# A four-layer graph network: the last attention layer in 32-column tiles, and a moved blank write

## Chip, core and metric

The kernel runs on one core of a Trainium2 chip. The metric is the time of one launch on the device, in microseconds. The core has five engines with an instruction queue each: TensorE (PE, matmuls, with weight loads shown as PEld), VectorE (DVE), ScalarE (ACT), GpSimd (POOL) and SyncE (SP). SP, ACT and POOL also issue DMA transfers, in the order in which these stand in their queues.

## What is computed

3125 nodes with 256 features pass through four layers; each adds a graph step and a mixing step to the nodes, then a feed-forward step. The change touches the end: the feed-forward step of layer 2, which picks two of eight experts for all nodes from the mean of the features, and layer 3. The reference of layer 3, cut:

```python
xn = _layernorm(x)
x = x + relu(gat(xn, edge_index, W, att_src, att_dst)) + mix(xn)
x = x + experts(x)          # one of 8 experts per node, with a capacity

def gat(x, edge_index, W, att_src, att_dst):
    xp = (x @ W).reshape(n, 4, 64)
    e = leaky_relu(a_src[src] + a_dst[dst], 0.2)      # per edge and head
    e_exp = exp(e - segment_max(e, dst)[dst])
    alpha = e_exp / segment_sum(e_exp, dst)[dst]
    return segment_sum(alpha * xp[src], dst)          # 4 heads of 64
```

## The kernel before

The 3125 nodes lie in 25 blocks of 125 (`P`, `NB`). `PIECES` groups them in six pieces of 500 nodes (`PW`) and one of 125. All arithmetic named here is in f32. `bank()` hands out four PSUM banks in turn.

A scheduler orders the instructions of each engine from the order in the code and from priorities; a pool's buffers and data dependencies decide the waits.

**Layer 2's feed-forward** (`l2_ffn`, L1779). The mean over all nodes is reduced (L1789), multiplied by the router weight `wr` (L1794), two softmaxes and a top-2 on VectorE and ScalarE follow, SP loads the two expert numbers into registers, and then each expert's weights (L1821 to L1825). `expert` multiplies all nodes by them; `y` takes up each block's result on VectorE (L1018). `wr` is loaded by SP, behind the weights of layer 3's mix.

**The blank write** (`l3_ffn`, L2168 on). Layer 3's experts read their nodes from `bx`, a table in DRAM of 3912 slots of 514 values, 8 MB. Before anything is scattered to it, it is filled with blank rows (L2190 and L2192, on ScalarE's queue) from a buffer named `row`. The name has one buffer, which the router of layer 3 uses later; the first such use is a copy of the nodes' numbers into it (L2253), which has no other input and so may stand early in VectorE's queue.

**The graph layer** (`l3_dense`, L1915). The edges are kept as a table of counts, sources by targets. The attention weights of one block of sources and one head for up to 1000 targets (two pieces) are made densely: ScalarE computes `t` (L1965), VectorE multiplies by the counts `cs` and gives `z` (L1968). TensorE multiplies `z` with the block's features: the stationary operand is `xr`, 64 features of the head and a column of ones, 65 columns; it accumulates 65 rows by 500 targets in one bank per head and piece (L1971). The last row is the sum of the weights. A pass over the 25 blocks for two heads and two pieces is called a half-turn here; there are six, and one turn for the last piece with all four heads. One block of a half-turn is a step: two `t`, two `z`, four matmuls. After a half-turn the sums are copied out, turned with small transposes of 65 rows (L1987), and per block divided and added to `x` (`finish`, L1925 to L1932).

`z` has three buffers, `t` two, `cs` three. The four banks of the accumulators are used again by the next half-turn.

**Beside it runs the mix** (`l3_mix_by_pieces`), interleaved by `together`, which always takes the part that has come less far. It is first keys and values for all blocks, then seven pieces of projections, normalisation and a small feed-forward part. When graph layer and mix have both finished a piece, `arrive` counts it down and calls `follow` (in `l3_ffn`, L2200 on), which normalises the nodes, routes them and scatters them to `bx` (L2255); the graph layer does so at step 5 of the next turn. Then the eight experts run.

Of the kernel before, what the change touches and what calls it, by code (L numbers as in the profile page):

```python
# [12 lines left out]
F32 = mybir.dt.float32  # L13
# [10 lines left out]
N = 3125  # L24
# [81 lines left out]
EARLY = 0.25  # L106
PIECES = [(i, min(PW, N - i)) for i in range(0, N, PW)]


class Net:  # L110
# [106 lines left out]

    def expect(self, parts, follow=None, lag=0):

        self.waiting = {i: parts for i, _ in PIECES}  # L220
        self.follow = follow or self.norm_turn_piece
        self.lag, self.due = lag, []

    def arrive(self, i):
        self.waiting[i] -= 1
        if self.waiting[i] == 0:
            self.due.append(i)
            while self.due and (len(self.due) > self.lag or not any(self.waiting.values())):
                i = self.due.pop(0)
                self.follow(i, min(PW, N - i))  # L230
# [1545 lines left out]
    def l2_ffn(self):  # L1776
        nc, tc, a = self.nc, self.tc, self.a
        NE = 8
        with ExitStack() as s:  # L1779
            sb = s.enter_context(self.pool("f2_sb"))  # L1780
            wk = s.enter_context(self.pool("f2_wk", 2))
            wr = self.load_w(sb, "L2_ffn_Wr")
# [35 lines left out]
            for j in range(2):  # L1818
# [6 lines left out]
                nc.sync.dma_start(b1, a["L2_ffn_b1"][ds(e, 1)].rearrange("o p f -> (o p) f"))  # L1825
# [11 lines left out]
    def l3_gnn_mix(self, before, arrivals):  # L1837
# [6 lines left out]
        with ExitStack() as s:  # L1844
# [12 lines left out]
            xr = sb.tile([P, NB, 4, 65], F32, name="xr")  # L1857
            nc.gpsimd.memset(xr[:, :, :, 64:65], 1.0)
            al = sb.tile([P, NB, 8], F32, name="al")
            for b in range(NB):  # L1860
                ps = self.bank()
                self.mm_tok(ps[:P, :264], self.xt, b, wx)
                nc.vector.tensor_copy(xr[:, b, :, :64], ps[:P, :D].rearrange("p (h d) -> p h d", h=4))
# [51 lines left out]
    def l3_dense(self, sb, wk, pa, xr, us, r_d):  # L1915

        nc = self.nc
# [3 lines left out]
        at = free[:65, 8 * PW:12 * PW].rearrange("p (h d) -> p h d", h=2)  # L1921

        def finish(b, h0, nh, acc):

            nc.vector.tensor_scalar(few[:, b, h0:h0 + nh], acc[:, :, 64], 1e-20, None, op0=OP.is_lt)  # L1925
            rd = wk.tile([P, 4], F32, name="rd")
            nc.vector.tensor_scalar(rd[:, :nh], acc[:, :, 64], 1e-20, None, op0=OP.max)
            nc.vector.reciprocal(rd[:, :nh], rd[:, :nh])
            t = wk.tile([P, 4, 64], F32, name="tf")
            nc.vector.tensor_mul(t[:, :nh], acc[:, :, :64], rd[:, :nh, None].to_broadcast([P, nh, 64]))  # L1930
            v = self.x[:, b, h0 * 64:(h0 + nh) * 64]
            nc.vector.scalar_tensor_tensor(v, t[:, :nh].rearrange("p h d -> p (h d)"), 0.0, v,  # L1932
                                           op0=OP.max, op1=OP.add)

        def target_rows(i, h0):

            n = min(2 * PW, N - i)
            for h in (h0, h0 + 1):
                if n > 0:
                    self.move(nc.sync, rows[:P, h, :n], r_d[h, i:i + n].partition_broadcast(P))  # L1940

        done, there = 0, []
        for h0 in (0, 2):
            target_rows(0, h0)
        for p0 in range(0, len(PIECES), 2):
            pcs = PIECES[p0:p0 + 2]
            n = sum(w for _, w in pcs)
            hg = 4 if n < PW else 2
            for h0 in range(0, 4, hg):
                acc = {}  # L1950
                for h in range(hg):
                    for k in range(len(pcs)):
                        acc[h, k] = pa.tile([65, 512], F32, name=f"acc{h * len(pcs) + k}")
                for b in range(NB):
                    cs = wk.tile([P, 2, PW], BF, name="cs", bufs=3)
                    if len(pcs) == 2:
                        self.move(nc.sync, cs, self.ctt_d[p0:p0 + 2, :, b, :].rearrange("k p d -> p k d"))
                        c = cs.rearrange("p k d -> p (k d)")
                    else:
                        self.move(nc.sync, cs[:, 0, :n], self.ctt_d[p0, :, b, :n])  # L1960
                        c = cs[:, 0, :n]
                    for h in range(hg):
                        k4 = h0 + h
                        t = wk.tile([P, 2 * PW], F32, name="t5")
                        nc.scalar.activation(t[:, :n], rows[:, k4, :n], AF.Relu, bias=us[:, 2, b, k4:k4 + 1],  # L1965
                                             scale=us[:, 0, b, k4:k4 + 1])
                        z = wk.tile([P, 2 * PW], F32, name="z", bufs=3)
                        nc.vector.scalar_tensor_tensor(z[:, :n], t[:, :n], us[:, 1, b, k4:k4 + 1], c,  # L1968
                                                       op0=OP.add, op1=OP.mult)
                        for k, (i, w) in enumerate(pcs):  # L1970
                            nc.tensor.matmul(acc[h, k][:, :w], xr[:, b, k4, :], z[:, k * PW:k * PW + w],  # L1971
                                             start=(b == 0), stop=(b == NB - 1))
                        done += n
                    yield done / (NB * N * 4)
                    if b == 5:
# [3 lines left out]
                if hg == 2:  # L1979
                    target_rows(pcs[0][0] + 2 * PW, h0)  # L1980
                    for h in range(2):
                        for k, (i, w) in enumerate(pcs):
                            self.evac(at[:, h, k * PW:k * PW + w], acc[h, k][:, :w])
                    for j in range(n // P):
                        ps = self.bank()
                        for h in range(2):
                            nc.tensor.transpose(ps[:P, h * 65:(h + 1) * 65], at[:, h, j * P:(j + 1) * P],  # L1987
                                                self.ident[:65, :65])
# [12 lines left out]
        for i in there:  # L2001
            self.arrive(i)
# [422 lines left out]
```

## Time and profile before

| | us |
|---|---|
| median of three runs | 4667.59 (4659.35 to 4668.40) |
| the profiled execution | 4666.18 |
| its span, first to last instruction | 4664.40 |

| stage of the profiled execution | us from the start |
|---|---|
| layers 0 to 2 up to the last gather matmul | 0 to 3251 |
| last transposes, mean, router, expert weights | 3251 to 3299 |
| layer 2's experts and layer 3's projections | 3299 to 3533 |
| graph layer 3 with its mix | 3533 to 4395 |
| its last turn, with 125 targets | about 4313 to 4395 |
| routing of the last piece, to the last scatter | 4395 to 4409 |
| layer 3's experts | 4409 to 4664 |

How to read the lines: a group has line, engine, operation, out<-in with shapes, count, then busy time, mean time of one, the idle time of the engine just before them and what released it. PE records of successive matmuls overlap, since a matmul's record reaches to its end while the next one has begun. A line of the windows has the stretch, its length, the busy time and count of each engine, the granted clock of TensorE, the share of DMA time and GB/s.

### The profile page before, as it was taken

How to read it: one execution, taken by the hardware profiler on the slowest of the kernel's cores; microseconds unless marked ns; L12 is line 12 of the kernel's file. 1: busy time of each engine (PE TensorE's matmuls, PEld its weight loads, DVE VectorE, ACT ScalarE, POOL GpSimd, SP SyncE). 2: the span in 40 equal slices, each digit the busy share in tenths (PEclk: the TensorE clock that was granted, in tenths of full speed). 3: DMA queues.
4: the chain of work that ended last, by engine and by line, in shares of the span. 5: the costliest groups of instructions: out<-in, count | busy, mean ns of one | idle time of the engine just before them, and what ended most of it. 6: DMA issues, size and time to landing. Idle time of an engine off the chain costs nothing. (4 is left out here: it accounts for less than half of the span.)

```text
span 4664.4 us, 50401 instructions
## 1 busy us (share of the span) xinstructions
PE 3722.3 (80%) x16695; PEld 2505.9 (54%) x16695; DVE 2505.6 (54%) x8604; ACT 1302.8 (28%) x2336; POOL 1020.2 (22%) x1041
## 2 busy tenths in 40 slices
PE   1887796499938799999656566766799999999698
PEld 0676695277724556555545455655464444444466
DVE  5877317544475526994322323444265666777544
ACT  1367100022213223323100000000155655555521
POOL 2000000400055000000577777775000000000011
PEclk9786896599959799999877777887899999999699
DMA  6244630244332000000333333334102222221232
GB/s 176 75 113 118 138 82 22 81 135 140 107 85 40 4 29 9 13 14 7 106 105 106 104 104 104 104 104 139 58 7 59 59 63 56 63 52 49 74 107 68
DMA packets 256035, 358.86 MB, mean 77 GB/s; under 512 B 62719, under 2 KB 199350, under 8 KB 255765
## 3 DMA queue, kind: packets, MB, share of 16 engines
q1 hardware_dynamic: 135900, 176.07, 13.1%
q0 software_dynamic: 62832, 126.93, 10.3%
q10 hardware_dynamic: 57033, 52.54, 4.2%
q8 instruction: 136, 2.23, 0.2%
q14 instruction: 134, 1.10, 0.1%
HBM read 268.73 MB, written 94.97 MB: 78 GB/s over the span
## 5 line engine op out<-in xcount | busy, mean ns | idle before, releaser
L1601 POOL DMA_INDIRECT hg<-hx_d,idx x782 | 743.3, 950 | 282.8 <-issue 214.2
L1617 PE MATMUL acc<-hg,to 128*125 128x256 f32 x2042 | 584.5, 449 | 197.9 <-DVE to L1612 192.8
L1617 PEld LDWEIGHTS acc<-hg,to 128*125 128x125 f32 x2042 | 455.4, 227 | 309.3 <-DVE to L1612 216.3
L1971 PE MATMUL acc<-z,xr 125*65 125x500 f32 (+1 forms) x1400 | 577.4, 556 | 14.3 <-DVE z L1968 13.0
L1965 ACT ACTIVATE t<-xn,us 125x1000 f32<-125x1000 f32 (+1 forms) x400 | 409.4, 1037 | 239.0 <-DVE z L1968 228.1
L1968 DVE SCALAR_TENSOR_TENSOR z<-t,us,cs 125x1000 f32<-125x1000 f32 (+1 forms) x400 | 409.3, 1028 | 115.5 <-PE acc L1971 92.6
L1971 PEld LDWEIGHTS acc<-z,xr 125*65 125x65 f32 x1400 | 188.9, 145 | 314.8 <-issue 265.5
L1605 DVE TENSOR_TENSOR kw<-hg,awt 128x8 f32<-128x8 f32 x98 | 16.4, 168 | 581.2 <-DMA hg<-hx_d,idx 513.2
L261 PE MATMUL ps<-xt,w 128*128 128x500 f32 (+1 forms) x672 | 269.0, 547 | 1.8 <-DMA w<-in_L_ffn_W_dram 1.8
L1612 DVE TENSOR_SCALAR to<-iota_w,rel_b,kw 128x125 f32<-128x125 f32 (+1 forms) x782 | 245.2, 383 | 35.6 <-PE acc L1617 28.7
L1536 DVE SCALAR_TENSOR_TENSOR junk<-iota_w,rel_b,lock 128x125 f32<-128x125 f32 (+1 forms) x782 | 248.1, 386 | 0.0
L2255 POOL DMA_INDIRECT bx_d<-row,slot x25 | 31.2, 1248 | 891.3 <-ACT t L1965 422.9
L589 PE MATMUL ps<-y,cb 125*125 125x256 bf16 x1875 | 214.7, 279 | 0.0
L589 PEld LDWEIGHTS <-cb 125*125 125x125 bf16 x1875 | 213.5, 141 | 0.1
L797 ACT ACTIVATE k<-k 125x128 f32<-125x128 f32 x50 | 15.9, 318 | 687.0 <-DVE k L796 686.9
L190 ACT ACTIVATE rstd_t<-rstd_t 125x4 f32<-125x4 f32 (+2 forms) x86 | 17.2, 203 | 645.8 <-DVE rstd_t L189 630.2
L255 PE MATMUL ps<-wo,h 128*125 128x256 f32 x800 | 187.7, 386 | 3.6 <-ACT h L1439 2.6
L243 PE MATMUL ps<-ident,xn 125*128 125x125 f32 x300 | 58.8, 347 | 159.8 <-DVE xn L209 159.7
L1445 DVE SCALAR_TENSOR_TENSOR x<-ps,lg,x 125x256 f32<-125x256 f32 x200 | 92.7, 480 | 173.6 <-PE ps L255 173.6
L261 PEld LDWEIGHTS ps<-xt,w 128*128 128x128 f32 x672 | 122.7, 193 | 114.7 <-issue 102.4
L261 PE MATMUL ps<-h,w 128*128 128x500 f32 (+1 forms) x448 | 179.5, 541 | 2.3 <-ACT h L1434 1.6
L255 PEld LDWEIGHTS ps<-wo,h 128*125 128x125 f32 x800 | 142.9, 187 | 65.9 <-ACT h L1439 43.7
(566 smaller groups left out, 6326.7 us busy)
## 6 DMA issues: line engine op xcount, KB each, us to landing
cs<-ctt_d SPq DMA_DIRECT2D x150, 218.8 KB
w<-in_L_ffn_w_dram SPq DMA_DIRECT2D x52, 512.0 KB
cnt_d<-cd SPq DMA_DIRECT2D x25, 683.6 KB
cb<-cnt_d SPq DMA_DIRECT2D x25, 683.6 KB
ctt_d<-ct ACTq DMA_DIRECT2D x6, 2734.4 KB
hg<-hx_d,idx POOLq DMA_INDIRECT x782, 2.8
b0x_d<-zero SPq DMA_DIRECT2D x1, 9984.0 KB
xb<-b0x_d SPq DMA_DIRECT2D x26, 384.0 KB
```

What stands on the lines that cost most here:

```text
L243: self.nc.tensor.transpose(ps[:, j * P:(j + 1) * P], src[:, i // P + j, h * 128:(h + 1) * 128], self.ident[:P, :P])
L255: self.nc.tensor.matmul(ps, xt[:, h, b * P:(b + 1) * P], w[:, h, :], start=(h == 0), stop=(h == k - 1))
L261: self.nc.tensor.matmul(ps, w[:, h, :], xt[:, h, i:i + n], start=(h == 0), stop=(h == k - 1))
L589: nc.tensor.matmul(ps[:P, :D], cf[k][:, h * P:(h + 1) * P], y3[:, b0 + k, j, :], start=(k == 0 and j == 0), stop=(k == m - 1 and j == 2))
L1445: nc.vector.scalar_tensor_tensor(self.x[:, b, :], ps[:P, :D], g[:, b, e:e + 1], self.x[:, b, :], op0=OP.mult, op1=OP.add)
L1536: nc.vector.scalar_tensor_tensor(junk[:, :m * P], self.iota_w[:, :m * P], rel[:, c:c + 1], lock[:, b:b + m].rearrange("p b n -> p (b n)"), ...
L1601: nc.gpsimd.indirect_dma_start(out=hg[:, j, :], out_offset=None, in_=hx, in_offset=bass.IndirectOffsetOnAxis(ap=idx[:, c0 + j:c0 + j + 1], ...
L1612: nc.vector.tensor_scalar(to, self.iota_w[:, :nb * P], rel[:, c:c + 1], kw[:, j:j + 1], op0=OP.is_equal, op1=OP.mult)
L1617: nc.tensor.matmul(acc[k], to[:, (k - b) * P:(k - b + 1) * P], hg[:, j, :D], start=(c == first[k]), stop=(c == last[k]))
L1965: nc.scalar.activation(t[:, :n], rows[:, k4, :n], AF.Relu, bias=us[:, 2, b, k4:k4 + 1], scale=us[:, 0, b, k4:k4 + 1])
L1968: nc.vector.scalar_tensor_tensor(z[:, :n], t[:, :n], us[:, 1, b, k4:k4 + 1], c, op0=OP.add, op1=OP.mult)
L1971: nc.tensor.matmul(acc[h, k][:, :w], xr[:, b, k4, :], z[:, k * PW:k * PW + w], start=(b == 0), stop=(b == NB - 1))
```

## The change

Transfers. The router weight of layer 2 is loaded by ScalarE's queue instead of SP's. The blank write becomes a function that is called in `l2_ffn` after the second expert's weights are issued, on SP's queue, with an order-only dependency that keeps it behind them. The second weight matrix of layer 3's expert 1 goes from ScalarE's queue to SP's.

Graph layer. The 65-column matmul with its column of ones is replaced. `xr` has 64 columns per head; each head's 64 columns are two tiles of 32, placed at columns 0, 32, 64, 96 of the array for two heads, so that one row of four matmuls gives the 128 outputs of two heads for one piece. A second row does the other piece. A third row of four has 32 columns of ones as stationary operand and gives the sums. A step is so 12 matmuls in three rows in place of 4, into three banks of 128 rows. The matmuls of a step are chained by order-only dependencies, each behind the one before, the first behind all `z` of the step; every third step (`BURST`) also behind a matmul of other work that stood last three rows of steps (`LAG`) earlier; and they have a higher priority. `z` has four buffers; `t` moves to a part of `xn` that is free. The sums are copied out as three times 128 rows and turned in transposes of 128, and `finish` treats four blocks at once.

Follow. It is cut in three by two `yield`s; the graph layer calls the next part at steps 1, 5, 9, 13, 17 and 21 (`next_part`), and what is left at the end runs at once.

```diff
+BURST, LAG = 3, 3
...
     def arrive(self, i):
...
-                self.follow(i, min(PW, N - i))
+                self.parts_due.append(self.follow(i, min(PW, N - i)))
+                if not self.by_parts:
+                    while self.parts_due:
+                        self.next_part()
+
+    def next_part(self):
+
+        if self.parts_due:
+            n = len(self.nc.cur_bb.bb.instructions)
+            if next(self.parts_due[0] or iter(()), self) is self:
+                self.parts_due.pop(0)
+            self.behind.update(i.name for i in self.nc.cur_bb.bb.instructions[n:])
...
-            wr = self.load_w(sb, "L2_ffn_Wr")
+            wr = self.load_w(sb, "L2_ffn_Wr", eng=nc.scalar)
...
-                nc.sync.dma_start(b1, a["L2_ffn_b1"][ds(e, 1)].rearrange("o p f -> (o p) f"))
+                last = nc.sync.dma_start(b1, a["L2_ffn_b1"][ds(e, 1)].rearrange("o p f -> (o p) f"))
+                if j == 1 and self.blank_slots:
+
+                    for ins in self.blank_slots():
+                        tc.add_manual_dep(ins, last.ins.name, mybir.DependencyInfo(
+                            mybir.DependencyClass.NoSync, mybir.DependencyReason.DATA), reason="weights first")
...
+        def finish(b, nb, h0, nh, acc):
+
+            w, nu = nb * P, len(acc) - 1
+            at = wk.tile([128, 3, PW], F32, name="at", bufs=1)
+            for k in range(nu + 1):
+                self.evac(at[:, k, :w], acc[k][:, :w])
...
+                units = [(h0, k, w) for h0 in hs for k, (_, w) in enumerate(pcs)]
+                acc = [pa.tile([128, 512], F32, name=f"acc{(turn + j) % 4}") for j in range(3)]
...
-                        t = wk.tile([P, 2 * PW], F32, name="t5")
...
-                        z = wk.tile([P, 2 * PW], F32, name="z", bufs=3)
...
-                            nc.tensor.matmul(acc[h, k][:, :w], xr[:, b, k4, :], z[:, k * PW:k * PW + w],
-                                             start=(b == 0), stop=(b == NB - 1))
...
+                        z = zs[h] = wk.tile([P, 2 * PW], F32, name="z", bufs=4)
...
+                    if steps % BURST == 0:
+                        marks.append(next((i for i in reversed(nc.cur_bb.bb.instructions)
+                                           if i.engine == mybir.EngineType.PE and i.name not in own | self.behind), None))
+                        if len(marks) > LAG and marks[-1 - LAG] is not None:
+                            made.append(marks[-1 - LAG])
+                    steps += 1
+                    with self.tc.high_priority(600):
+                        for out, left, h0, j, k, w, q in (
+                                [(acc[u], xr[:, b, h0 + j, f:f + 32], h0, j, k, w, 64 * j + f)
+                                 for u, (h0, k, w) in enumerate(units) for j in range(2) for f in (0, 32)]
+                                + [(acc[2], self.ones[:P, :32], h0, j, k, w, 64 * u + 32 * j)
+                                   for u, (h0, k, w) in enumerate(units) for j in range(2)]):
+                            mm = nc.tensor.matmul(out[q:q + 32, :w], left, zs[h0 + j][:, k * PW:k * PW + w],
+                                                  start=(b == 0), stop=(b == NB - 1), tile_position=(0, q))
+                            for i in made:
+                                self.tc.add_manual_dep(mm.ins, i.name, row, reason="in one row")
+                            made = [mm.ins]
+                            own.add(mm.ins.name)
...
+                    if b % 4 == 1:
+                        self.next_part()
...
-            nc.scalar.dma_start(bx[:whole].rearrange("(t p) d -> p t d", p=112),
-                                blank[:112, 0, None, :].to_broadcast([112, whole // 112, WX]))
-            nc.scalar.dma_start(bx[whole:], blank[:NE * CAP - whole, 0])
+
+            def blank_slots():
+                self.blank_slots = None
+                return [nc.sync.dma_start(bx[:whole].rearrange("(t p) d -> p t d", p=112),
+                                          blank[:112, 0, None, :].to_broadcast([112, whole // 112, WX])).ins,
+                        nc.sync.dma_start(bx[whole:], blank[:NE * CAP - whole, 0]).ins]
...
-                w2 = self.load_w(wk, "w2", a["L3_ffn_w2"][e], eng=nc.scalar)
+                w2 = self.load_w(wk, "w2", a["L3_ffn_w2"][e], eng=nc.sync if e == 1 else nc.scalar)
```

## The prediction

> **What bounds the kernel now.** I read the busy slices of the page first, then windows over the last third of the span, then the groups of instructions of the stage that they single out, and last the waits of the one stretch in which TensorE stands still.
>
> The slices: each digit is a fortieth of the 4664.40 us span, 116.6 us.
> ```profile
> PE   1887796499938799999656566766799999999698
> DVE  5877317544475526994322323444265666777544
> PEclk9786896599959799999877777887899999999699
> ```
> TensorE is full from the thirtieth to the thirty-seventh slice, 3381 to 4314 us, at full clock; from 3533 on this is the last graph layer with its mix. Around the border of the slices before (3150 to 3381) it dips.
>
> Windows over the stage, columns busy time and count per engine, clock, DMA share, GB/s:
> ```profile
> core 0: us, PE busy (x) PEld busy (x) DVE busy (x) ACT busy (x) POOL busy (x), PEclk, DMA share, GB/s
> 3533.00:3750.00 217.00, 216.82 (x624) 88.82 (x623) 140.55 (x205) 138.12 (x173) 0.00 (x0) 1.00 0.21 57
> 3750.00:4000.00 250.00, 243.32 (x758) 111.70 (x757) 179.39 (x401) 137.52 (x145) 10.40 (x8) 0.98 0.22 61
> 4000.00:4250.00 250.00, 244.90 (x769) 113.76 (x768) 176.35 (x397) 137.63 (x148) 10.07 (x8) 0.99 0.20 52
> 4250.00:4330.00 80.00, 76.54 (x240) 32.30 (x238) 61.03 (x120) 53.73 (x63) 0.00 (x0) 0.96 0.24 63
> ```
> Of these 797 us TensorE works 782, VectorE 557, ScalarE 467. So TensorE is the bound, and what is taken from it counts until VectorE's 557 come near.
>
> The costs of the layer's loop, from the groups of the page:
> ```profile
> L1971 PE MATMUL acc<-z,xr 125*65 125x500 f32 (+1 forms) x1400 | 577.4, 556 | 14.3 <-DVE z L1968 13.0
> L1965 ACT ACTIVATE t<-xn,us 125x1000 f32<-125x1000 f32 (+1 forms) x400 | 409.4, 1037 | 239.0 <-DVE z L1968 228.1
> L1968 DVE SCALAR_TENSOR_TENSOR z<-t,us,cs 125x1000 f32<-125x1000 f32 (+1 forms) x400 | 409.3, 1028 | 115.5 <-PE acc L1971 92.6
> ```
> The code calls this matmul 700 times and the trace has 1400 records: an f32 matmul is two passes. Twenty of them in a row take 8.55 us in the timeline (3699.51), so a pass starts every 0.42 us and a 500-column matmul costs 0.84 us. VectorE waits for TensorE to give z back (92.6 us), hardly the other way (13.0).
>
> The stretch with TensorE idle, by its windows and its waits:
> ```profile
> 3255.00:3260.00 5.00, 0.00 (x0) 0.00 (x0) 0.09 (x1) 0.00 (x0) 0.00 (x0) 0.50 1.05 345
> 3265.00:3270.00 5.00, 0.00 (x0) 0.00 (x0) 0.00 (x0) 0.00 (x0) 0.00 (x0) 0.50 1.05 371
> ```
> ```profile
> PE ps L1794 <- DMA L_ffn_Wr<-in_L_ffn_Wr_dram: 28.4, 1, 28.4
> ACT xt L165 <- DMA b<-in_L_ffn_b_dram: 25.1, 1, 25.1
> DVE row L2253 <- DMA bx_d<-row: 24.2, 1, 24.2
> ```
> The 8 MB of blank slots (L2190, issued at 3244.5) fill all DMA engines until 3279. Three engines stand behind them: ScalarE at its small loads, VectorE at a copy into the blank's buffer, TensorE at the router weight.
>
> **What the Trainium skill says.** "TensorE: Matmul & The Clock Gate", Part 3, section "Measured speedup vs the span model", gives 2.38x for three column tiles of 32 at 512 columns; its section "The mechanism" says that matmuls start and end strictly in program order. The two pull apart here, since two passes of one f32 matmul go to the same tile. "TensorEngine Tiling (Array Packing)", "Key Properties", says that tiles work independently and that changing the mode drains the array. The trace of before has no column tiles, so it shows none of this; it does show passes in order, one at a time.
>
> **The change part by part.** Sums are against the profiled execution, 4666.18 us with a span of 4664.40; the median shown is 4667.59, 1.4 us more, which I add at the end.
>
> *Transfers.* The blank write moves from ScalarE's queue to SP's, behind both experts' weights; the router weight moves from SP's queue to ScalarE's, ahead. The last transposes before the mean end at 3254.8. The ScalarE copy of their result then runs at about 3255.5 instead of 3277.8, the mean at 3256 instead of 3279.8. The router weight is issued when the last gather matmuls end (3251) and small loads land in some 3 us, so it is no later than the mean. Everything to the expert's first matmul (3299.5) hangs on the mean and keeps its distances: 24 us gone. The mix weights on SP, 2.6 MB, need about 8.5 us at the 305 GB/s seen here and are done at 3257; a later gamma or beta load may hold ScalarE's exponential by 1 or 2 us. The blank is issued at about 3275 and needs 8 MB / 0.35 = 23 us behind 2 MB of expert weights: done near 3305. Queued behind it on SP are only the first count tiles and rows, needed at 3500. The VectorE copy into the blank's buffer now stands after the eighth expert result, 3328.3 - 24 = 3304, so it waits 0 to 3 us, which four PSUM banks can hide. Gain 24 us, between 20 and 27.
>
> *Second weight of expert 1, moved to SP behind its first.* It leaves the 12 us (4411 to 4423) in which expert 0's first inputs arrive at 301 GB/s; 1 MB less is 3 us. Taken: 2.5 us, from 0 to 3.5.
>
> *Tiles.* Six half-turns of 25 steps, 150 steps. Before: 4 matmuls x 0.84 = 3.35 us a step. After: 12 matmuls of 32 columns in 3 rows of four. If four tiles run beside each other, a row costs one matmul, 0.84, a step 2.51, and 150 steps give 126 us. If each pass waits for the one before it in its own tile and holds up the row behind it, pass one of a tile runs beside pass two of the previous tile: 0.42 us per matmul, 5.03 a step, 252 us lost. I take the first, because tiles that were queued behind each other's passes would not be independent; the second stays as a rival. The last turn (25 steps of 125 columns) is set by ScalarE's four activations of 0.49 us each, 1.95 a step, against 0.86 of matmuls; no change.
>
> *Mode changes.* In the compiled order TensorE's accumulating matmuls stand in 81 runs, where before they stood in 157. Two changes of mode per run are 162; a drain is the difference of a matmul's length, 582 ns, and its pitch, 419: 0.163. 26 us lost, between 0 and 40.
>
> *VectorE and ScalarE.* Per half-turn eight blocks of five operations (0.142 + 0.147 + 0.157 + 0.288 + 0.289) go, 8.2 us, and four evacuations of 65 rows become three of 128, at the same length per row of 500. In come about 0.5 us for the sums and, for each of two units, a small copy (0.15), a multiply and an add over 512 elements (0.69 each by the slope from 0.29 at 128 to 0.42 at 256): 3.6 us. Six times 4.6 is 28 us off VectorE: 557 becomes 529 against a stage of about 690. Off the path, but the load grows from 70 to 77%.
>
> *Rows of three steps.* This is the added wait. z has four buffers, two steps. VectorE makes a step's two z in 2 x 1.255 = 2.51 us, just TensorE's new pace, so the third step of a run can wait for its z, and all that is queued behind on TensorE (the mix) with it; and a mix matmul that waits for normalisation (about 5 us of VectorE for four blocks) has only two or three steps of tiles as cover, 5 to 7.5 us, in which VectorE also owes z. Before, the cover was the slower matmuls. Fifty runs at 0 to 1 us each: I take 25 us, bounds 0 and 60.
>
> *Follow in three parts.* It moves router work of about 10 us per piece to later steps. Pieces that arrive at step 5 have parts at steps 9, 13, 17, 21, so in the last turn two parts of one piece fall after the loop, up to 8 us between the last z (4394.6) and the last scatter (4408.0). In return the last 25 steps, which took 82 us where ScalarE's activations need 49, lose some of their VectorE load. Net 0, from -10 to +8.
>
> Sum: -24 - 2.5 - 126 + 26 + 25 = -101.5. 4666.2 - 101.5 = 4564.7, and with 1.4 for the median 4566.
>
> **The rivals.**
> A. Tiles side by side, gain eaten: rows of four at 0.95 or more (its 24 small weight loads a step, or partial overlap), and TensorE waits 60 us for z. Then the tiles give 0 to 40 and the transfers carry it: 4666 - 26 - 20, some 4620, up to 4690. For it: VectorE pace equals the new TensorE pace. Against: VectorE has 23% of the stage free.
> B. Slower: the two passes queue in their tile. +252 - 26.5 + 0.5 x 26 (drains; waits for z vanish under the longer runs) is +238: 4905. It decides from 0.279 us per tile matmul (3.35 / 12), a third above full overlap (0.209). For it: strict order; passes of one matmul follow each other directly in the trace. Against: tiles that hold their own weights.
> C. The tiles stay fully serial, 12 x 0.84 = 10 us a step, a change that doesn't do what it says: +1000 us, 5650. The 2.38x of the skill speaks against it.
>
> **How the numbers follow.** Forecast case 0.68, its own range 4500 to 4620. A 0.17, of which 0.11 faster, 0.03 same, 0.03 slower. B 0.14, C 0.01. A measurement of this kernel tells 0.2%, 9 us, from no change. Faster 0.79, same 0.03, slower 0.18. The low end is no loss to drains or waits and the full transfers, 4667.6 - 26.5 - 126 = 4515, less 15 for the tail and for idle time in the stage; the high end takes in A to 4680. Left out are B, C and the edges.
>
> **What would show it.** Right: about 2100 calls of the accumulating matmul, four starting within a few ns of each other, a row every 0.84 us; TensorE busy again by 3260 with the mean; the stage at about 720 us. Wrong: starts 0.42 us apart in a row (B); VectorE waits near zero and TensorE waiting for z over 60 us (A); an idle stretch that stays at 3255, or VectorE standing at the blank's buffer later.

## The result, and the profile after

| | us | ratio to before, 95% interval |
|---|---|---|
| before, median of 4 runs | 4665.11 (4659.35 to 4668.40) | 1 |
| after, median of 4 runs | 4612.67 (4607.15 to 4617.31) | 0.9887 [0.9872, 0.9903] |
| forecast | 4566 (4500 to 4680) | |

The change makes the kernel 52 us faster, and the forecast had 101. Between the two profiled executions it is 49 us (spans 4664.40 and 4615.44), and it lies here:

| stage | before, us | after, us | difference |
|---|---|---|---|
| start to the dense layer's first matmul | 3533.5 | 3515.9 | -17.6 |
| six half-turns | 785.8 | 743.8 | -42.0 |
| last turn, to its last `z` | 75.3 | 70.3 | -5.0 |
| last `z` to the last scatter | 13.4 | 29.8 | +16.4 |
| last scatter to the end | 256.4 | 255.7 | -0.7 |

The last turn is counted here from TensorE's first matmul of it, which was at 4319.3 us before. The stage list ahead and the prediction count it from about 4313, where ScalarE's first activation of it ran, and so have 82 us for it.

First the busy slices of the page of after, which answer to those of before.
```profile
PE   1887797499928789999766666776799999998598
DVE  6877317544474625994422323344356676676444
PEclk9786897599958789999877777888899999999699
```
VectorE stands at 6 and 7 tenths in the dense stage, as it did before, and TensorE still shows 9 nearly everywhere. In tenths, the lost time is not to be seen. It shows in windows over the same stage (columns as before: stretch, length, busy time and count of PE, PEld, DVE, ACT, POOL, clock, DMA share, GB/s).
```profile
3255.00:3260.00 5.00, 0.43 (x2) 0.20 (x2) 2.38 (x10) 1.75 (x3) 0.00 (x0) 0.74 0.97 321
3265.00:3270.00 5.00, 0.00 (x0) 0.00 (x0) 5.00 (x9) 0.00 (x0) 0.00 (x0) 0.50 0.08 29
...
3750.00:4000.00 250.00, 232.32 (x1487) 100.93 (x1486) 176.48 (x353) 139.10 (x147) 10.38 (x8) 0.96 0.23 60
4000.00:4250.00 250.00, 236.24 (x1500) 104.86 (x1498) 170.67 (x337) 138.87 (x155) 13.53 (x8) 0.97 0.19 50
```
Of the two 5 us stretches, the second was full of DMA (1.05) and empty of work before; now the DMA engines are free (0.08) and VectorE is busy for all of it. Of 500 us in the half-turns TensorE was idle 11.8 before (243.32 + 244.90 busy); now it is idle 31.4. VectorE is busy for 522 of the 744 us, which is 70% (before 546 of 786).

The groups of the layer, from the page (line, engine, operation, busy time, mean ns of one, idle time before them):
```profile
L2005 DVE SCALAR_TENSOR_TENSOR z<-xn,us,cs 125x1000 f32<-125x1000 f32 (+1 forms) x400 | 400.1, 1027 | 112.7 <-PE acc L2021 62.9
L2021 PE MATMUL acc<-z,xr 125*32 125x500 f32 (+1 forms) x2800 | 381.5, 560 | 28.7 <-DVE z L2005 27.6
L2021 PE MATMUL acc<-z,ones 125*32 125x500 f32 (+1 forms) x1400 | 226.6, 551 | 0.0
```
That is 4200 records for 2100 calls, two passes each, as before. A run of tiles in the timeline shows that they lie beside each other (start, length, engine, line):
```profile
3708.78 1.88 PE L2021 MATMUL acc<-z,xr 125*32 125x500 f32 x16
3710.48 1.02 PE L2021 MATMUL acc<-z,ones 125*32 125x500 f32 x8
3711.32 1.44 PE L2021 MATMUL acc<-z,xr 125*32 125x500 f32 x12
```
From 3708.78 to 3711.32 there are 24 passes, or 12 matmuls, in 2.54 us: a row of four takes 0.85 us, what one matmul of 500 columns took before. The single records start at 3708779, 786, 792 and 799 ns; then the second passes of the same four tiles start at 3709222, 229, 236 and 242.

And the waits in the half-turns (engine, line, what was waited for: us, times, longest), TensorE before, TensorE after, VectorE after:
```profile
PE acc L1971 <- DVE z L1968: 3.6, 6, 0.8
PE ps L1340 <- DVE o L1328: 2.6, 1, 2.6
```
```profile
PE acc L2021 <- DVE z L2005: 13.6, 10, 5.5
PE ps L1354 <- DVE o L1342: 7.6, 10, 1.5
PE ps L2077 <- DVE o L2114: 5.5, 1, 5.5
```
```profile
DVE np_st L2109 <- PE ps L269: 55.6, 34, 7.5
DVE z L2005 <- PE acc L2021: 52.8, 48, 8.8
```
TensorE waits for VectorE's `z` and for VectorE's results in the mix, both more than before. VectorE waits for TensorE in two places: at the statistics of the mix's normalisation (`np_st`, 48.7 us before) and for a `z` buffer to come back (92.2 us before). Each is late for the other by turns, and each has idle time.

For what follows I split the half-turns by the records of TensorE: from the start of each matmul to the start of the next one, counted under **tiles** where the first is a matmul of the graph layer and under **others** where it is not.

| half-turns, us | before | after |
|---|---|---|
| accumulating matmuls, 'tiles' | 515.2 | 434.9 |
| other matmuls | 270.7 | 308.9 |

150 steps of three rows with two passes at 0.419 us are 377 us, so tiles stand 58 us above it; before, 1200 passes at 0.419 were 503, and the measured time stood 12 above that. And the others, which are nearly the same work, grew by 38.

### The profile page after: what moved, and what is told of

Its sections match the earlier page's. It is cut to its first block, busy times and chain, and to the rows that moved or that the text cites. A ratio compares the mean times of both kernels' runs of the same rounds, so it can differ in the third digit from the quotient of the medians.

```text
span 4615.4 us, 55679 instructions
## 1 busy us (share of the span) xinstructions
PE 3660.6 (79%) x19470; PEld 2461.5 (53%) x19470; DVE 2481.3 (54%) x8419; ACT 1293.0 (28%) x2330; POOL 1023.8 (22%) x1040
## 5 line engine op out<-in xcount | busy, mean ns | idle before, releaser
L2005 DVE SCALAR_TENSOR_TENSOR z<-xn,us,cs 125x1000 f32<-125x1000 f32 (+1 forms) x400 | 400.1, 1027 | 112.7 <-PE acc L2021 62.9
L2002 ACT ACTIVATE xn<-xn,us 125x1000 f32<-125x1000 f32 (+1 forms) x400 | 404.8, 1037 | 163.6 <-DVE z L2005 160.4
L2021 PE MATMUL acc<-z,xr 125*32 125x500 f32 (+1 forms) x2800 | 381.5, 560 | 28.7 <-DVE z L2005 27.6
L1619 DVE TENSOR_TENSOR kw<-hg,awt 128x8 f32<-128x8 f32 x98 | 16.4, 168 | 582.1 <-DMA hg<-hx_d,idx 507.3
L2021 PE MATMUL acc<-z,ones 125*32 125x500 f32 (+1 forms) x1400 | 226.6, 551 | 0.0
L2021 PEld LDWEIGHTS acc<-z,xr 125*32 125x32 f32 x2800 | 102.9, 112 | 230.3 <-issue 129.3
```

Source lines behind the costliest of these rows:

```text
L2002: nc.scalar.activation(t[:, :n], rows[:P, h, :n], AF.Relu, bias=us[:, 2, b, h:h + 1], scale=us[:, 0, b, h:h + 1])
L2005: made.append(nc.vector.scalar_tensor_tensor(z[:, :n], t[:, :n], us[:, 1, b, h:h + 1], c, op0=OP.add, op1=OP.mult).ins)
L2021: mm = nc.tensor.matmul(out[q:q + 32, :w], left, zs[h0 + j][:, k * PW:k * PW + w], start=(b == 0), stop=(b == NB - 1), tile_position=(0, q))
```

## The experiments

A kernel with a ratio was timed against the kernel before on the same chip; of the others there is a single time, beside before's 4663.5 to 4665.6 on the same chip. The four kernels that have two `slot` buffers ran on two chips on which the kernel before takes 4809 and 4802 us, so of these only ratios and stages are compared.

### The transfers alone

```diff
-            wr = self.load_w(sb, "L2_ffn_Wr")
+            wr = self.load_w(sb, "L2_ffn_Wr", eng=nc.scalar)
```
This is the kernel before with the three moved transfers, this line among them, and the old graph layer.

> The kernel before with the three moved transfers alone. My theory (the transfers give their 24 us in full and the rest of the change gives the other half of what was measured): 4640 us, that is 24 to 27 below before, TensorE's idle stretch after 3255 gone, VectorE not held at the copy into the blank's buffer. Rival (the blank write now collides later, or other work takes the time back before the last layer): less than 15 us gained, so that the tiles would have given nearly all of the 52 us.

4640.48 us against 4665.59, ratio 0.9946 [0.9934, 0.9958], which is 25 us. The dense layer's first matmul is at 3508.5 (3533.5 before), the half-turns 783.3, the tail 13.4 as before. The transfers do what was said, and the graph layer and its follow-up bring the rest, some 27 of 52 us.

### Tile by tile in place of rows

```diff
-                                [(acc[u], xr[:, b, h0 + j, f:f + 32], h0, j, k, w, 64 * j + f)
+                                sorted([(acc[u], xr[:, b, h0 + j, f:f + 32], h0, j, k, w, 64 * j + f)
...
-                                   for u, (h0, k, w) in enumerate(units) for j in range(2)]):
+                                   for u, (h0, k, w) in enumerate(units) for j in range(2)], key=lambda m: m[-1])):
```
The same twelve matmuls of a step, ordered so that the three of one tile follow each other.

> The changed kernel with the twelve matmuls of a step in another order: the three of one column tile behind each other, then the next tile. Same work and same outputs. Theory S (matmuls start strictly in program order and only the two passes of a row of four are interleaved): the six passes of a tile follow each other, a step takes two to four times as long, the time rises by 300 us or more. Theory W (each tile takes its matmuls from a window in its own order): the time stays within 30 us of the changed kernel.

4799.85 us; half-turns 935.0, with tiles at 635.9. Neither expectation holds: the order costs 191 us of half-turns, neither 300 nor 30. The timeline of this kernel shows what is left of the overlap:
```profile
3704.86 1.89 PE L2021 MATMUL acc<-z,xr 125*32 125x500 f32 x6
3706.56 0.58 PE L2021 MATMUL acc<-z,ones 125*32 125x500 f32 x1
...
3707.42 0.58 PE L2021 MATMUL acc<-z,ones 125*32 125x500 f32 x1
3707.45 0.61 PE L2021 MATMUL acc<-z,xr 125*32 125x500 f32 x2
```
Inside a run, three passes start every 0.43 us here, one of the ones and two of features, where rows of four start four every 0.419. So the order in rows matters. It is no queue in strict order either: the order that the code's dependencies ask for has two matmuls of features, four passes, ahead of the first one with ones, and six passes have started before it. TensorE begins with the next tile while a matmul of this one still waits, but here never has more than three tiles at work; which rule limits it the trace does not show.

### One z for two heads

```diff
+                        if h % 2:
+                            zs[h] = zs[h - 1]
+                            continue
-                        t = spare[h % 2]
+                        t = spare[b % 2]
```
Leaves out the activation and the `z` of every odd head; its matmuls use the even head's `z`.

> The changed kernel, but z is made for the even heads only and used for both, so the activation and the VectorE product of every odd head are left out; TensorE's work is the same. Theory (the lost part of the tiles' gain is VectorE: rows wait for z, and mix matmuls wait for a VectorE that is behind): the six half-turns fall from 744 us to 670 or less, the time to 4540 or less. Rival (mode changes and the order on TensorE itself cost it): the half-turns stay above 720 us and the time above 4585.

4549.91 us; half-turns 690.0, tiles 386.7, others 303.3. In between for the time, clear in its parts: the tiles come within 10 us of 377, so what they lack is `z`. The others keep 303 of 309, so most of their growth is not `z`. Halving `z` also lets four buffers reach over four steps in place of two, so that this run does not tell VectorE's throughput from the depth of its buffers. The fifth buffer below does.

### Shorter and longer runs of tiles

```diff
-BURST, LAG = 3, 3
+BURST, LAG = 1, 9
```
and, in the second kernel, 6 and 2.

> Rows of one step: the order behind other work is asked for at every step (BURST 1) and looks nine steps back (LAG 9), the same distance of nine steps. Same computation. Reference point is the changed kernel's profile: six half-turns 744 us, of which tile matmuls 435 (377 if no row ever waited or split) and other matmuls 309 (271 before the change). Theory: a run of tiles longer than the two steps that four z buffers hold must wait for VectorE, so that shorter runs cut the tiles' excess (58 us), while each added run costs two mode changes at about 0.19 us together. Up to 70 more runs cost 13 us; the tiles' excess falls to 35 or less; the mix's waits of 30 us stay, as VectorE has the same work. The time is then within 15 us of the changed kernel's 4613. Rival: the mix's waits come from the runs' being bunched, so other matmuls fall below 290 us and the time below 4590.

> Rows of six steps (BURST 6, LAG 2). Same computation. Theory: six steps of tiles need 15 us of TensorE and twelve z, of which four are ready; VectorE makes one in 1.26 us if it does nothing else, so each run's second half waits whenever VectorE also has work of the mix. Fewer runs save at most 8 us of mode changes; the tile part rises from 435 to 455 or more and the time by 10 us or more, to 4625 or above. Rival: the changes of mode and the short cover are what costs, so that the time falls, to 4605 or less.

| half-turns, us | tiles | others | sum | runs of tiles |
|---|---|---|---|---|
| one step: 4624.16 in all | 424.7 | 325.4 | 750.1 | 98 |
| three steps (after) | 434.9 | 308.9 | 743.8 | 75 |
| six steps: 4632.18 in all | 428.9 | 326.8 | 755.7 | 66 |

Both are a little slower. The expected numbers for the tiles failed, 424.7 where 412 or less was expected, and 428.9 where 455 or more was; what one part gains, the other loses or more. The edits changed the real runs less than their names say: 150 steps in 98, 75 and 66 runs are 1.5, 2.0 and 2.3 steps each. Within that range the length of the runs is not what costs the time, and three steps is a fair choice among these; longer runs were not made.

Both times are within what the theory said (4598 to 4628, and 4625 or above), for another reason than it gave. After also gives the change of mode. From the last tile matmul of a run to the next other matmul it is 512 ns where 419 is the pitch, and on the way back 202 or 309 where the other matmul's own pitch is 107 or 215: about 95 ns each way. 75 runs in the half-turns have 150 changes, so 14 us. Counted from the first of the four tiles of a run's last row, which start over 20 ns, the way out is 113 ns, and the sum is then 16.

### The mix turns data that is ready

```diff
-                self.nc.tensor.transpose(ps[:, j * P:(j + 1) * P], o[:, j, h * 128:(h + 1) * 128], self.ident[:P, :P])
+                src = self.xt[:P, h, j * 128:(j + 1) * 128] if o is None else o[:, j, h * 128:(h + 1) * 128]
+                self.nc.tensor.transpose(ps[:, j * P:(j + 1) * P], src, self.ident[:P, :P])
```
and the same for the second set of transposes of the mix.

> Leaves the dependence of the mix's two sets of transposes on VectorE out: they turn features that have long been ready (xt) in place of the attention output and of the normalised rows (o); VectorE still computes both. Theory: of the 38 us by which the other matmuls of the half-turns grew, about 28 are TensorE standing at these two places (gaps behind the transposes of o and behind the multiplication by Wm), and TensorE is the bound, so the other matmuls fall from 309 to 285 us or less and the time by 15 us or more, to 4598 or below. Rival: VectorE's pace is what sets the half-turns, so a wait removed there comes back as a wait for z: other matmuls fall, the tiles' 435 rise by as much, and the time stays within 6 us of the changed kernel's 4613.

4594.93 us, 17.7 below after; half-turns 724.2 (-19.6), others 294.8 (-14.1), tiles 429.4. The others stay above the 285 of the theory, but the time falls as it said and the rival's 6 us is excluded. The waits of TensorE in this kernel's half-turns:
```profile
PE acc L2022 <- DVE z L2006: 13.0, 7, 6.8
PE ps L1355 <- DVE o L1342: 2.5, 3, 1.5
```
The wait for `o` after the attention (L1342) falls from 7.6 to 2.5 us, the 5.5 us at the second transposes are gone, and the wait for `z` has not grown. So part of the others' growth, 14 of 38 us, is TensorE standing at the mix's own chain, which the slower accumulation had nearly covered (2.6 us of such waits before).

### Parts three steps apart

```diff
-                    if b % 4 == 1:
+                    if b % 3 == 1:
```

> The changed kernel with the parts of what follows an arrival three steps apart in place of four, so that six parts (both pieces) fit behind step 5 of the last turn. Theory (two parts of one piece fall behind the last turn, and the last piece then waits for the one row buffer until that piece's four scatters have landed): last z to last scatter falls from 29 us to 13 to 16, the time by 10 to 14, to 4600. Rival (the tail is long for another reason, such as the larger evacuations of the last turn, or the work only moves into the last turn): under 4 us.

4605.49 us, ratio 0.9863 [0.9849, 0.9878]. The stretch from the last `z` to the last scatter falls from 29.8 to 13.8 us, as before the change; but the last turn takes 80.4 us in place of 70.3, for the two parts now run in it. The 16 us of the tail were these parts, and 10 of the 16 come back in the loop. The time is 7 us below after, between the two expectations, and the intervals of the two ratios overlap.

### A row buffer, then a slot buffer, for the last piece

```diff
-                row = wk.tile([P, 4, WX], F32, name="row")
+                row = (wk.tile([P, 4, WX], F32, name="row") if nb > 1 else
+                       self.xn.rearrange("p b d -> p (b d)")[:, 200:200 + WX].rearrange("p (j c) -> p j c", j=1))
...
-                slot = wk.tile([P, 4], I32, name="slot")
+                slot = wk.tile([P, 4], I32, name="slot", bufs=2)
```
The first kernel has the first edit alone, the second both. Of after, the timeline of the tail shows why (in brackets the idle time before and who released it):
```profile
4344.20 1.19 POOL L2308 DMA_INDIRECT bx_d<-row,slot  x1 [44.32 <-issue]
...
4348.69 1.19 POOL L2308 DMA_INDIRECT bx_d<-row,slot  x1 [0.30 <-issue]
4351.48 0.41 DVE L210 TENSOR_SCALAR row<-x,ln_mv,ln_rs 125x256 f32<-125x256 f32 x1 [8.14 <-DMA bx_d<-row,slot]
...
4359.75 1.19 POOL L2308 DMA_INDIRECT bx_d<-row,slot  x1 [9.87 <-issue]
```
The loop's last `z` was at 4329.91. Two parts of piece 5 still follow, its four scatters go from 4344.2 to 4348.7, and only then can the last piece write the one `row`.

> The last piece's normalised rows go to a free part of xn (514 columns of rows that the last turn does not use) in place of the one buffer named row; all else as in the changed kernel, parts four steps apart. Theory: the last piece stands 8 us at that buffer, which the four scatters of the piece before still read, so the stretch from the last z to the last scatter falls from 29.8 us to 18 to 24, the last turn stays at 71, and the time falls by 6 to 12 us. Rival: the parts of piece 5 that run after the loop hold the engines, not the buffer; then the stretch stays above 26 and the gain is under 4 us.

> As last_piece_own_row, and the slot numbers, which the scatters read too, have two buffers. With the own row alone the stretch from the last z to the last scatter was 24.1 us, and VectorE stood 4.84 us at the slot buffer for the scatters of the piece before. Theory: that buffer is the next in line; the stretch falls to 18 to 21 us, the last turn stays at 71, and the time is 8 to 14 us below the changed kernel's 4612.7, at some 4602. Rival: the scatters themselves run one behind the other on GpSimd (five of them 1.5 us apart), so that the last cannot go sooner; the stretch stays at 23 or more and the time within 6 us of the changed kernel's.

With its own row the stretch is 24.1 us and the ratio 0.9886 [0.9869, 0.9902], no gain that can be told. The next buffer stands in its place; the timeline of the kernel with its own row:
```profile
4356.35 0.16 DVE L2305 TENSOR_TENSOR slot<-pos,over 125x1 int32<-125x1 f32 x1 [4.84 <-DMA bx_d<-row,slot]
```
With both it is 21.8 us, a little above the 18 to 21 expected, and now the last piece's scatter follows the four others on GpSimd at the same distance as these have, 1.5 us:
```profile
4489.30 1.19 POOL L2309 DMA_INDIRECT bx_d<-xn,slot  x1 [0.31 <-DMA bx_d<-row,slot]
```
The ratio is 0.9867 [0.9848, 0.9886]. Its interval overlaps that of after, so that the gain in time is not shown, only the 8 us in the trace.

### The end of the mix on GpSimd

```diff
-            nc.vector.tensor_mul(o[:, :nb], o[:, :nb], g2[:P, None, :].to_broadcast([P, nb, D]))
+            nc.gpsimd.tensor_mul(o[:, :nb], o[:, :nb], g2[:P, None, :].to_broadcast([P, nb, D]))
```
and the two additions behind it likewise, on top of the kernel with row and slot.

> As last_piece_own_row_and_slot, and the three operations over 1024 elements that end a piece of the mix (times g2, plus b2, added to x; 7 each, 1.1 us of VectorE each, 23 us in all) go to GpSimd, which is idle there. Theory: what the half-turns lack is VectorE's time, either as a late z or as a late operand of the mix, and TensorE follows it in part: of 23 us less on VectorE some 5 to 15 come out of the half-turns (744 us in the changed kernel), and the time is that much below the run beside it. Rival: VectorE has 30 per cent of the half-turns free and these three operations come when nobody waits, so that the gain is under 3 us; or GpSimd takes so long or slows VectorE so much that the time rises.

Ratio 0.9933 [0.9917, 0.9950], so 0.66% slower than without the edit; half-turns 767.6 against 741.1. The rival's second half holds. The timeline of this kernel, VectorE and then GpSimd:
```profile
3901.48 12.29 DVE L2005 SCALAR_TENSOR_TENSOR z<-xn,us,cs 125x1000 f32<-125x1000 f32 x5
```
```profile
3901.80 3.16 POOL L2091 TENSOR_TENSOR o<-o,L_mix_g 125x1024 f32<-125x1024 f32 x1 [507.91 <-DVE o L2114]
3905.04 3.22 POOL L2092 TENSOR_TENSOR o<-o,L_mix_b 125x1024 f32<-125x1024 f32 x1
3908.34 3.21 POOL L2094 TENSOR_TENSOR x<-x,o 125x1024 f32<-125x1024 f32 x1
```
Five `z` alone need some 6 us and 12.29 here: three of them have a record of 3.37 us in place of 1.25, and each ends about 1.05 us after one of the GpSimd operations does, as if it had begun only then. The Trainium skill, "SBUF — State Buffer", section "SBUF: two separate sides", says that a VectorE operation with two SBUF inputs and a GpSimd operation that reads SBUF lock each other out of a shared port pair for the whole instruction; this trace agrees. `z` has `t` and `cs` as inputs and is held, while a copy out of PSUM in the middle of a GpSimd operation (4279.71 to 4282.92) keeps its length, 672 ns as the median:
```profile
4280.61 0.67 DVE L164 COPY at<-acc 128x500 f32<-128x500 f32 x1
```
The GpSimd operations are held too: of those over 1024 elements in the half-turns, the four that did not begin while a `z` ran took 2.35 to 2.39 us, not 3.2. Over the 300 large `z` the mean rises from 1253 to 1347 ns, 28 us, more than the 23 taken off VectorE.

### A fifth z buffer

```diff
-                        z = zs[h] = wk.tile([P, 2 * PW], F32, name="z", bufs=4)
+                        z = zs[h] = wk.tile([P, 2 * PW], F32, name="z", bufs=5)
...
-                t = wk.tile([P, 4, 2, 64], F32, name="tf")
+                t = wk.tile([P, 4, 2, 64], F32, name="tf", bufs=1)
...
-                    xt = wk.tile([128, HB, P], F32, name="xtp", bufs=2)
+                    xt = wk.tile([128, HB, P], F32, name="xtp", bufs=1)
```

> As last_piece_own_row_and_slot, with five z buffers in place of four; the room is taken from tf and xtp, which get one buffer each. VectorE stands some 50 us of the half-turns at z for a buffer that TensorE still reads, and TensorE stands for z at other times: each waits for the other by turns. Theory: what the half-turns lack is not VectorE's throughput but how far it may run ahead, so a fifth buffer cuts the tiles' excess (433 to 435 us against 377) to 35 us or less and the half-turns from 741 to 731 or less, and the time is 8 us or more under that of last_piece_own_row_and_slot relative to the kernel before (ratio 0.985 or less). Rival: VectorE's order, in which z stands behind operations that wait for the mix's matmuls, sets it, and a buffer more only moves the wait; half-turns within 5 us of 741, ratio 0.9855 to 0.988. Against both: one tf and one xtp stall finish and the router and the time rises.

Ratio 0.9832 [0.9818, 0.9847] against 0.9867 of the same kernel with four; half-turns 719.0 against 741.1, tiles 401.6 against 432.9. The theory holds in all three numbers; the intervals of the two ratios just miss each other, and the two kernels ran on different chips, so that the 22 us of the half-turns are the firmer number. The waits of TensorE in the half-turns, first with four buffers, then with five:
```profile
PE acc L2021 <- DVE z L2005: 14.9, 11, 6.3
PE ps L1354 <- DVE o L1342: 7.1, 9, 1.5
PE ps L2077 <- DVE o L2114: 5.5, 1, 5.5
```
```profile
PE ps L1354 <- DVE o L1342: 13.6, 8, 7.4
PE ps L2077 <- DVE o L2114: 6.6, 1, 6.6
...
PE acc L2021 <- DVE z L2005: 1.7, 4, 0.7
```
The wait for `z` is nearly gone with the same VectorE work (522 us busy in the half-turns with four buffers, 521 with five). The wait for `o` has grown from 7.1 to 13.6: 9 of the 31 us gained in the tiles are lost in the others, 308.2 to 317.5. The order on TensorE changed too, to 65 runs of tiles from 75; but the kernel with six steps has 66 runs, and its tiles took 428.9, so that the number of runs doesn't explain the 31 us.

> As five_z, with the parts of what follows an arrival three steps apart instead of four. In the four-apart kernel the last turn took 71 us and the stretch to the last scatter 22 with its own row and slot; three apart and without these it took 81 and 14. Theory: with three apart the two parts run inside the loop and the own row and slot then gain nothing more, so last turn and tail are together 92 to 95 us, as in the four-apart kernel, and the time is within 6 us of five_z. Rival: the last turn has idle time to take the two parts in once z runs one buffer further ahead; together 88 us or less, and the time is 5 us or more below five_z.

Ratio 0.9821 [0.9806, 0.9837], the best of all. Half-turns are 716.2 us; last turn and tail are together 89.6 us, as in the kernel with parts four apart (also 89.6), between the two expectations, and the distance of the parts makes no difference there any more. The interval leaves open whether it is faster than with four apart; it does not meet that of after (from 0.9872), nor that of the kernel with parts three apart and four `z` buffers (from 0.9849), which has no own row and slot either. Against the latter the half-turns fall by 24 us as well (740.3 to 716.2), here 13 in the tiles and 11 in the others: what the fifth buffer gives in all comes out again, and how it divides depends on the order.

## Why the prediction came out as it did

**Transfers, -24.** Right. From the last block of the gathers to the expert's first matmul it was 48.5 us and is 25.1, so 23.4 less, and the transfers alone brought 25 us. Nothing else took the place: VectorE does not stand at the blank's buffer. One step of it did not come: the router weight is issued at 3255.6 and not at 3251, and TensorE starts its multiplication 4.2 us after the mean is there (3258.7 to 3262.9). It had stood 3.0 us before, so that the distance from the mean was nearly kept all the same. Of the dense start 17.6 remain, because in the profile of after the gathers end 3.1 us later, and the distance from the last copy of `xr` to the first dense matmul is 22.1 us in place of 18.9.

**Second weight of expert 1, -2.5.** The stretch behind the last scatter is 0.7 us shorter. With the transfers alone it was 257.4, 1.0 longer than before, so that no gain of this term is shown. It was not tried alone.

**Tiles, -126.** Right: four side by side, a row at the price of one matmul. The prediction weighed the strict program order of starts in the Trainium skill ("TensorE: Matmul & The Clock Gate", Part 3, "The mechanism") against independent tiles; the trace decides for the latter: the second passes of four tiles come behind the first passes of all four, and in the kernel ordered by tile a matmul of the next tile starts ahead of one that stands before it in the code, which differs from the page. The rival in which two passes of a matmul queue in their tile would need starts 0.42 us apart inside a row, and they are 7 ns apart.

**Mode changes, +26.** The direction was right, and the size was well above what it is. A change costs about 95 ns, not 163, and 150 of them in the half-turns are 14 to 16 us. The estimate took the difference of a record's length and the pitch for the drain, and the trace does not bear that out.

**VectorE, -28.** Near: its busy time in the half-turns fell by 24 us, from 546 to 522. Its share stayed at 70% and did not go to 77%, because the stage stayed longer than forecast.

**Rows of three steps, +25 (0 to 60).** This is the step that failed, by its size and not by its kind. The waits took about 68 us, above its upper bound. Of the tiles' 58 us above 377, 8.5 are at the ends of runs (75 changes of mode at 113 ns) and 49 are put down to late `z`; before, 12 lay above, so 37 more. Part of these are gaps, part are rows that start with two tiles in place of four, one head ahead of the other: of 900 passes of rows, 147 start in two halves more than 150 ns apart in after, none with one `z` for two heads, 28 with five `z`. The others grew by 38, of which 7 are changes of mode, so 31 more. 126 - 16 - 37 - 31 is 42, as measured; the two waits are what is left by subtraction, so that this sum closes of itself.

The prediction named both waits and then priced them together as one guess per run, 50 runs at half a microsecond, though it counted 81 runs itself. It also put them down to rows of three steps, but with runs of 1.5, 2.0 and 2.3 steps the half-turns differ by 12 us at most, and the ones in the middle are the best. What the experiments put in its place is two things. For the tiles it is the depth of `z`: with five buffers 30 of the 47 us of late `z` go, at the same VectorE load. The prediction used VectorE's free share as the argument against waits, and that share says nothing of when a `z` can be made: VectorE stands 55.6 us at the mix's statistics and 52.8 for a buffer. That it owes `z` after these stops is argued from the waits and not shown by itself. For the mix it is the loss of its cover: with operands that are ready 14 of the others' 31 us go, and 5.5 of the tiles'. The other 17 are not separated; some are waits for other results of VectorE and ScalarE in the mix.

**Follow in three parts, net 0 (-10 to +8).** Mis-sized: the tail rose by 16.4 and the last turn fell by 5.0. The prediction saw the two parts that fall after the loop. It did not see that the last piece then queues behind their scatters for the single `row`, 8.14 us, and behind that for the single `slot`, 4.84. That the last turn is set by ScalarE's four activations also fell: at 70 us, and at 80 with two more parts in it, it takes more than the 49 of these, as it did before the change.

**Rival A** gave 4620 for overlap that is eaten by waits, and the time is nearer to it than to the forecast. Of its two mechanisms the rows at 0.95 are not there (0.84), and TensorE's wait for `z` is, but smaller: the sign given for it was over 60 us of that wait and hardly any waiting of VectorE, and the waits show 13.6 us (49 of late `z` by the split of the records), with 52.8 of VectorE for a buffer.

Put together: 24 + 126 were there as forecast; 68 of waits in place of 25 and 11 of last turn and tail in place of 0 are the difference, with 6 us of the transfers that these two profiles don't show. That the mode changes were priced at some 10 us too much hid part of it, which is luck.

## What to carry to other kernels

When the bounding engine is made faster up to the pace of its supplier, ask how many buffers the supplier may run ahead and which other waits stand in its queue; its busy share hides both, and here one buffer more was worth about a third of a per cent by the ratios. What the slow engine covered has to be priced on its own, too: the mix's own chain cost 2.6 us of waiting while the accumulation was slow, and 13.1 when it was fast. When work is cut in parts, count the parts that are left at the end of the loop, and the single buffers that the next piece shares with them.

## What the runs showed of the hardware that was not expected

- An f32 matmul's two passes do not stay together when four tiles are in line: four first passes 7 ns apart, then four second passes 0.42 us later; 12 matmuls of 32 columns by 500 take what three of full width take.
- Ordered by tile, three passes start every 0.43 us inside a run, not one and not four, and not in the order of the code; the tiles' part was 635.9 us in place of 434.9.
- A change between tiles and the full array cost about 95 ns each way (512 ns in place of 419, 202 or 309 in place of 107 or 215).
- GpSimd's operations over 1024 elements took 2.4 us where none began beside a `z` and 3.2 where it did, and a `z` beside one took 3.37 us in place of 1.25; a VectorE copy out of PSUM beside one kept its 0.67.
- Chips differ: on the two chips of the four kernels with two `slot` buffers the kernel before took 4802 and 4809 us against 4665. The extra time lies before the dense stage, which begins at 3656.4 us in the kernel with row and slot and at 3515.9 in after, while the half-turns take 741.1 and 743.8.
